# Two transformer layers in one kernel: a reordered opening of the first layer, and the last feed-forward pieces of the second layer spread over more turns

## The chip, the cores and the metric

The kernel runs on one core of one Trainium2 chip. Its time is the device time of one execution in microseconds (us); a kernel's figure is the median of its runs. The kernel before took 1442.1, 1445.23 and 1445.4 us, median 1445.23.

## The reference

`x` is 2048 tokens of width 128, in fp32. Two layers of the same shape follow one another, each with an attention part `s` and a feed-forward part `g`:

```
xn = layernorm(x)
s  = layernorm(xn + (relu_attention(xn) @ w_out + b_out)) * gamma + beta      # 16 heads of 8
g  = silu(routed_block(xn))
x  = x + s * g
xn = layernorm(x)
s  = causal_softmax_attention(xn, W_Q, W_K, W_V, W_O)                          # 16 heads of 64
g  = silu((silu(xn @ wg.T) * (xn @ wu.T)) @ wd.T)                              # hidden 384
x  = x + s * g

relu_attention: w = relu(q @ k.T / sqrt(8)); w / (sum(w) + 1e-6) @ v           # over all 2048 keys
routed_block:   the 255 tokens of highest router weight pass through a small transformer
                block and are written back scaled by that weight; the others pass unchanged
wg, wu, wd:     integers times 1/127
```

## The kernel before

**Engines and orders.** PE, ACT and DVE execute in the order in which the program is written (a manual schedule). POOL's and SP's (the DMA queue's) instructions are ordered by the Tile scheduler. Tokens are held as 16 chunks of 128 (`xin`, `xne`), taken together in four groups of 512.

**Opening of the first layer.** A group `i` is normalised by the generator `normalised(i)` in two parts. The first part takes the statistics on DVE (four pairs of `bn_stats`, `bn_aggr`) and the square root on ACT. The second takes the reciprocal and one Newton step, writes four chunks of `xne` (L895, all on DVE), transposes them on PE and copies the result on ACT (L102, L104). `begin()` runs this for the groups 0 and 1, with the projections of the keys of group 0 and of the first queries between them (`project`, L786: PE, then a rounded copy `high` on ACT and the remainder `low` added on DVE, L793), and the first values. All these projections are 512 columns wide. POOL meanwhile makes the copies of the weights that the projections read (L289 is one of its own for the routed block), and clears a buffer `nothing` of which SP later writes four copies to DRAM.

**Steps of the first layer.** The relu-attention runs in 256 steps, `n = 64 qc + 16 g + kb`: 512 queries `qc`, group of four heads `g`, block of 128 keys `kb`. A step issues four score matmuls (L948, one for each head of the group), four relus, each on ACT (L956) or DVE (L958) as a running account of work decides (`work.lesser`), and the products (L964) of the step two before. A group of heads needs its keys `kT[:, g]` for all 16 blocks. The keys of group 0 come straight from `project`; those of the groups 1 to 3 go in both halves (`high`, `low`) to DRAM (`spread`) and are read back by DMA into the rows where the scores want them. The rest of the opening is spread over the first steps by the tables

```
due = {
    0: (more_keys,), 1: (more, 2), 2: (all_keys, 2), 3: (more_values, 1), 4: (more, 3),
    5: (all_keys, 3), 6: (more_values, 2), 7: (all_keys, 1), 8: (all_queries, 0),
    9: (more_values, 3), 11: (all_keys, 0),
}
read = {9: (2, 1), 10: (3, 1), 12: (1, 1), 14: (0, 1)}
```

`more(i)` normalises group `i`, `all_keys(i)` makes its keys for all heads, `more_values(i)` its values, `more_keys` the keys of token group 1 for head group 0, and `read` starts the read-back of `kT`. A step that is not in `due` advances the generator `others()` instead: the routed block, then the second layer's feed-forward weights, then the end of each 512 queries. PSUM has six banks for scores and projections ("s"), one for those follow-ups that are not of that kind ("x"), and one accumulator.

**Turns of the second layer.** The causal attention runs in turns `r`, 19 for each of eight pairs of heads. A turn issues score matmuls (L1462), the masks and maxima on DVE (L1482, L1483), the exponentials on ACT (L1496), the transposes of the last turn's `p` (L1733), their evictions on ACT and DVE (L1740), and the weighing of the values (L1512). Into the turns a plan `ahead` puts the projections of keys (L1365), queries (L1415) and values (L1400) for coming turns. A projected key or query is copied by ACT (L1386) and split by POOL into a rounded part and a remainder (L1388, 64x512 casts, and L1390, subtractions).

**The last 512 tokens between the layers.** The feed-forward of the last 512 tokens isn't done before the turns begin. `tail()` lists its pieces, and the turn loop takes them one after the other: from turn 2 on one piece of arithmetic at the end of each turn (`first`, `gated`, `second`, `normal`), then from turn 6 on the pieces with a matmul in place of a projection (`turn` L1289, three gate and three up products L1294, `down` L1312). `first` and `second` take the moments of a tensor: statistics on DVE, then the inverse root from an integer first guess and four Newton steps of four small POOL instructions each (L1244 to L1248). `gated` has two parts of four DVE instructions: `y = (y - mean) * g` (L1267), then `xin = y * inv + xin` (L1271). `normal` writes the normalised tokens, which `turn` transposes.

Of the kernel before, what the change touches and what calls it, by code (L numbers as in the profile page):

```python
# [11 lines left out]
F32 = mybir.dt.float32  # L12
# [4 lines left out]
AF = mybir.ActivationFunctionType  # L17
# [5 lines left out]
P = 128  # L23
# [33 lines left out]
@with_exitstack  # L57
def mixed_layers_kernel(
    ctx: ExitStack,
    tc: tile.TileContext,  # L60
    a: dict,
    out: bass.AP,
):
    nc = tc.nc
    ctx.enter_context(nc.allow_non_contiguous_dma(reason="small weights and rows of sums"))

    const = ctx.enter_context(tc.tile_pool(name="const", bufs=1))
    small = ctx.enter_context(tc.tile_pool(name="small", bufs=4))


    ident = const.tile([P, P], F32, name="ident")
    make_identity(nc, ident)


    def row_load(name, n, pool):

        t = pool.tile([P, n], F32, name=f"row_{name}")
        nc.sync.dma_start(out=t, in_=a[name].partition_broadcast(P))
        return t


    xin = const.tile([P, NC, D], F32, name="xin")
    xn1T = const.tile([P, S], F32, name="xn1T")
    xsrc = a["x"].rearrange("(c p) d -> p c d", p=P)
    for i in range(NQ):
        nc.sync.dma_start(out=xin[:, 4 * i : 4 * i + 4, :], in_=xsrc[:, 4 * i : 4 * i + 4, :])


    with tc.manual_schedule(
        engines={mybir.EngineType.PE, mybir.EngineType.Activation, mybir.EngineType.DVE}  # L90
    ):
        second = layer1(ctx, tc, a, small, ident, xin, xn1T, row_load, out)
        layer0(ctx, tc, a, small, ident, xin, xn1T, row_load, second)
        for _ in second.turns:
            pass


def transposed(nc, psum, ident, src, dst, tag, bufs, copy):

    t = psum.tile([P, 4, P], F32, tag=tag, bufs=bufs, name="t")  # L100
    for i, s in enumerate(src):
        nc.tensor.transpose(t[:, i, :], s, ident)  # L102
    n = len(src)
    copy(dst, t[:, :n, :].rearrange("p a b -> p (a b)"))  # L104


def layer0(ctx, tc, a, small, ident, xin, xn1T, row_load, second):
    nc = tc.nc
# [11 lines left out]
    )  # L120
    nc.scalar.dma_start(
        out=w_qkv.rearrange("p g j t d -> p (g j t d)"), in_=a["w_qkv"]
    )

    w_k = keep.tile([P, 4, HD0, 4], F32, name="w_k")
    w_q = keep.tile([P, 4, HD0, 4], F32, name="w_q")
    for t, dst in ((1, w_k), (0, w_q)):
        for i in range(4):
            nc.gpsimd.tensor_copy(dst[:, :, :, i], w_qkv[:, 0, :, t, :])
# [9 lines left out]
    for n, bit in (("k", 2), ("q", 1)):  # L139
# [8 lines left out]
    w_out = end.tile([P, D], F32, name="w_out")  # L148
    nc.scalar.dma_start(out=w_out, in_=a["w_out"])
    b_out = row_load("b_out", D, end)  # L150
    gamma = row_load("gamma", D, end)
    beta = row_load("beta", D, end)
    router_w = keep.tile([P, 1], F32, name="router_w")
    nc.scalar.dma_start(out=router_w, in_=a["router_w"])
    router_b = row_load("router_b", 1, keep)
# [10 lines left out]
    rwb = rw.tile([P, KSEL], F32, tag="og", bufs=4, name="rwb")[:, :P]  # L166
    nc.gpsimd.tensor_copy(rwb, router_w.to_broadcast([P, P]))
    work = Work(nc)
    routed = routed_block(
        tc, a, work, rb, rw, dram, small, ps, ident, xne, xnT, g0, rwb, router_b, row_load,  # L170
        (b_out, gamma, beta, xin),
    )
# [45 lines left out]
def routed_block(  # L218
    tc, a, work, rb, rw, dram, small, ps, ident, xne, xnT, g0, rwb, router_b, row_load, rest
):  # L220
# [23 lines left out]
    yield  # L244

    tok = rb.tile([P, KSEL], BF16, name="tok")
    nc.gpsimd.iota(
# [515 lines left out]
def relu_attention(  # L763
# [18 lines left out]

    def project(dst, w, i, low):

        t = bank([P, 512], "s")
        nc.tensor.matmul(  # L786
            t, w.rearrange("p a d n -> p (a d n)"), xnT[:, 512 * i : 512 * i + 512],
            start=True, stop=True,
        )
        high = aw.tile([P, 512], F32R, tag="high", name="high")  # L790
        nc.scalar.copy(high, t)
        work.add(a=0.6, d=0.75)
        return lambda: nc.vector.scalar_tensor_tensor(dst, high, low, t, ALU.mult, ALU.add)  # L793

    def keys(i):
        return project(kT[:, 0, 512 * i : 512 * i + 512], w_k, i, low_k)

# [75 lines left out]

    def normalised(i):

        cs = range(4 * i, 4 * i + 4)
        st = small.tile([P, 4, 6], F32, tag="ln_st", name="ln_st")
        mv = small.tile([P, 4, 2], F32, tag="ln_mv", name="ln_mv")
        v = small.tile([P, 4], F32, tag="ln_v", name="ln_v")
        r = small.tile([P, 4], F32, tag="ln_r", name="ln_r")  # L880
        y = small.tile([P, 4], F32, tag="rs_y", name="y")
        t = small.tile([P, 4], F32, tag="rs_t", name="t")
        for k, c in enumerate(cs):
            nc.vector.bn_stats(st[:, k, :], xin[:, c, :])
            nc.vector.bn_aggr(mv[:, k, :], st[:, k, :])
        nc.vector.tensor_scalar(v, mv[:, :, 1], 1e-5, None, ALU.add)
        nc.scalar.activation(y, v, AF.Sqrt)
        yield
        nc.vector.reciprocal(y, y)
        nc.vector.tensor_tensor(t, y, y, ALU.mult)  # L890
        nc.vector.tensor_tensor(t, t, v, ALU.mult)
        nc.vector.tensor_scalar(t, t, -0.5, 1.5, ALU.mult, ALU.add)
        nc.vector.tensor_tensor(r, y, t, ALU.mult)
        for k, c in enumerate(cs):
            nc.vector.tensor_scalar(  # L895
                xne[:, c, 0:D], xin[:, c, :], mv[:, k, 0:1], r[:, k : k + 1],
                ALU.subtract, ALU.mult,
            )
        transposed(
            nc, ps, ident, [xne[:, c, 0:D] for c in cs], xnT[:, 512 * i : 512 * i + 512],  # L900
            "s", NS, nc.scalar.copy,
        )
        yield

    tokens = [normalised(i) for i in range(NQ)]

    def begin():

        next(tokens[0])
        next(tokens[1])  # L910
        next(tokens[0])
        k = keys(0)
        next(tokens[1])
        q = queries()
        k()
        next(tokens[2])
        q()
        values(0)
        work.a, work.d = 0.0, 3.0

    def more_keys():
        return keys(1)

    def more(i):

        next(tokens[i])
        work.add(a=0.6, d=2.0)
        if i + 1 < NQ:
            next(tokens[i + 1])
            work.add(a=0.2, d=1.8)  # L930

# [114 lines left out]
    def moments(src):  # L1046
# [18 lines left out]

    due = {
        0: (more_keys,), 1: (more, 2), 2: (all_keys, 2), 3: (more_values, 1), 4: (more, 3),
        5: (all_keys, 3), 6: (more_values, 2), 7: (all_keys, 1), 8: (all_queries, 0),
        9: (more_values, 3), 11: (all_keys, 0),
    }  # L1070
    read = {
        9: (2, 1), 10: (3, 1), 12: (1, 1), 14: (0, 1),
    }
# [17 lines left out]
    ends, steps, block = pools  # L1091
    ready, held, other, later = set(), [], others(), None
    begin()
    for n in range(n_steps + 2):
        if n < n_steps:
            held.append((n, scores(n)))
# [37 lines left out]
def layer1(ctx, tc, a, small, ident, x1, xn1T, row_load, out):  # L1134
# [94 lines left out]
    def moments(x):  # L1229
# [13 lines left out]
        nc.vector.tensor_scalar(yi, yi, -1.0, float(0x5F3759DF), ALU.mult, ALU.add)  # L1243
        for i in range(4):  # L1244
            nc.gpsimd.tensor_tensor(t, y, y, ALU.mult)
            nc.gpsimd.tensor_tensor(t, t, v, ALU.mult)
            nc.gpsimd.tensor_scalar(t, t, -0.5, 1.5, ALU.mult, ALU.add)
            nc.gpsimd.tensor_tensor(r if i == 3 else y, y, t, ALU.mult)  # L1248
        return mv, r

    def tail():
# [12 lines left out]
        def gated():  # L1264
            mv, r = got.pop()
            for c in range(4):
                nc.vector.scalar_tensor_tensor(  # L1267
                    y[:, c, :], y[:, c, :], mv[:, c, 0:1], g[:, c, :], ALU.subtract, ALU.mult
                )
            for c in range(4):  # L1270
                nc.vector.scalar_tensor_tensor(  # L1271
                    x[:, c, :], y[:, c, :], r[:, c : c + 1], x[:, c, :], ALU.mult, ALU.add
                )

        def second():
            got.append(moments(x))

        def normal():
# [38 lines left out]

        out = [(f, (), False) for f in (first, gated, second, normal)] + [(turn, (), True)]
        for n, later in (("w_gate", raw), ("w_up", times)):
# [341 lines left out]
    for pr in range(NP):  # L1661
# [5 lines left out]
        if pr == 0:  # L1667

            plan = [(0, values, 1)] + plan[6:]
        if pr == NP - 1:  # L1670
# [94 lines left out]
    def attention():  # L1765
# [10 lines left out]
        while r < len(turns) + 1 or todo or done or after:  # L1776
# [43 lines left out]
            for few in (r > 2, False, True, True)[: 4 if ending else 2]:  # L1820
# [5 lines left out]
                if f:  # L1826
                    f()
            if r >= 2 and pieces and not pieces[0][2]:
                g, args, _ = pieces.pop(0)
                g(*args)  # L1830
# [72 lines left out]
```

## Time and profile before

One profiled execution, whose own time is 1445.89 us; the span from its first to its last instruction is 1444.2 us. All rows below are of that execution.

| stretch of the span (us) | length | PE busy | DVE busy | ACT busy | POOL busy | granted clock |
|---|---|---|---|---|---|---|
| 0 to 18.59: up to the first scores | 18.59 | 6.83 | 13.26 | 4.58 | 9.51 | 1.00 |
| 18.59 to 43.99: steps 0 to 7 | 25.40 | 21.13 | 13.82 | 15.54 | 0.00 | 0.87 |
| 43.99 to 65.13: steps 8 to 15 | 21.14 | 19.02 | 12.26 | 12.38 | 0.00 | 1.00 |
| 65.13 to 505.00: the rest of the steps | 439.87 | 427.04 | 350.89 | 348.03 | 49.73 | 1.00 |
| 505.00 to 530.57: end of layer 1, turns 0 to 3 | 25.57 | 22.43 | 20.02 | 15.55 | 3.77 | 1.00 |
| 530.57 to 549.42: turns 4 and 5 | 18.85 | 12.60 | 15.46 | 8.04 | 9.34 | 0.82 |
| 549.42 to 1423.00: the other turns | 873.58 | 871.96 | 632.72 | 547.64 | 231.87 | 1.00 |
| 1423.00 to 1444.20: the end | 21.20 | 11.57 | 8.16 | 4.30 | 0.61 | 0.92 |
| whole span | 1444.20 | 1392.57 | 1066.60 | 956.05 | 304.83 | 0.993 |

A busy time counts the instructions that an engine executes, without register, branch, semaphore and DMA-issuing ones. The granted clock is the share of full speed at which TensorE was allowed to run in that stretch; a mean below 1 comes from windows at 0.50. In the timelines each line gives the start, the length, the engine and source line, the operation with the tile written and the tiles read, the shape, the number of instructions put together, and in brackets the idle time of the engine before it with what ended it.

### The profile page before, as it was taken

How to read it: one execution, taken by the hardware profiler on the slowest of the kernel's cores; microseconds unless marked ns; L12 is line 12 of the kernel's file. 1: busy time of each engine (PE TensorE's matmuls, PEld its weight loads, DVE VectorE, ACT ScalarE, POOL GpSimd, SP SyncE). 2: the span in 40 equal slices, each digit the busy share in tenths (PEclk: the TensorE clock that was granted, in tenths of full speed). 3: DMA queues.
4: the chain of work that ended last, by engine and by line, in shares of the span. 5: the costliest groups of instructions: out<-in, count | busy, mean ns of one | idle time of the engine just before them, and what ended most of it. 6: DMA issues, size and time to landing. Idle time of an engine off the chain costs nothing.

```text
span 1444.2 us, 26907 instructions
## 1 busy us (share of the span) xinstructions
PE 1392.6 (96%) x10070; PEld 845.5 (59%) x10070; DVE 1066.6 (74%) x1935; ACT 956.1 (66%) x2055; POOL 304.8 (21%) x414
## 2 busy tenths in 40 slices
PE   5999999999999979999999999999999999999997
PEld 2222333222222457777777777777777777777775
DVE  6588788788888476677768668768767767777775
ACT  4588787787888556666656666556656656666563
POOL 2001000150000121222232242242232232242210
PEclk9999999999999999999999999999999999999999
DMA  4432001111000311101111111011011111111110
GB/s 124 123 82 72 12 12 30 52 29 41 20 19 6 100 30 30 30 16 45 34 26 45 31 30 45 18 43 38 23 30 45 31 30 45 30 30 31 28 40 15
DMA packets 44065, 56.46 MB, mean 39 GB/s; under 512 B 11680, under 2 KB 26400, under 8 KB 43936
## 3 DMA queue, kind: packets, MB, share of 16 engines
q1 hardware_dynamic: 43120, 53.44, 14.6%
q8 instruction: 79, 1.29, 0.4%
q0 software_dynamic: 384, 1.05, 0.3%
q14 instruction: 50, 0.41, 0.1%
q10 hardware_dynamic: 432, 0.26, 0.1%
HBM read 27.74 MB, written 8.35 MB: 25 GB/s over the span
## 4 chain that ended last, share of the span: by engine, by line
PE 62%; ACT 1%; DVE 1%; issue 0%; ACTq 0%; DVEq 0%
PE t L1462 18%; PE z L1512 18%; PE t L1733 17%; PE m L1613 2%; PE m L1400 2%; PE m L1415 2%; PE m L1365 2%; ACT p L1496 1%; PE m L1294 0%; ACT pt L1740 0%; DVE xin L1271 0%; PE m L1312 0%; DVE zs L1596 0%; DVE res L1631 0%; ACT L1303 0%
## 5 line engine op out<-in xcount | busy, mean ns | idle before, releaser
L1483 DVE TENSOR_REDUCE tops<-t 128x1 f32<-128x1024 f32 (+4 forms) x320 | 334.6, 1062 | 98.9 <-PE t L1462 92.3
L956 ACT ACTIVATE rt<-t 128x512 f32<-128x512 f32 x597 | 315.5, 604 | 64.7 <-PE t L948 63.2
L1740 ACT COPY pt<-t 128x512 f32<-128x512 f32 (+3 forms) x359 | 163.4, 518 | 261.5 <-PE t L1733 260.3
L1496 ACT ACTIVATE p<-t,tops 128x1024 f32<-128x1024 f32 (+7 forms) x384 | 331.2, 883 | 7.8 <-DVE tops L1483 7.2
L958 DVE TENSOR_SCALAR rt<-t 128x512 f32<-128x512 f32 x427 | 275.7, 684 | 69.7 <-PE t L948 63.8
L1462 PE MATMUL t<-k,q 128*128 128x512 f32 (+4 forms) x1280 | 314.7, 389 | 9.4 <-ACT p L1496 9.3
L964 PE MATMUL t<-rt,va 128*9 128x512 f32 x2048 | 269.9, 600 | 4.3 <-ACT part L980 4.3
L1733 PE MATMUL t<-ident,p 128*128 128x128 f32 x2176 | 270.1, 275 | 2.6 <-ACT x L1386 1.4
L1512 PE MATMUL z<-pt,v 128*64 128x256 f32 (+1 forms) x2304 | 268.3, 374 | 0.5 <-ACT zs L1747 0.5
L1462 PEld LDWEIGHTS t<-k,q 128*128 128x128 f32 x1280 | 219.0, 189 | 83.2 <-issue 32.2
L1733 PEld LDWEIGHTS t<-ident,p 128*128 128x128 f32 x2176 | 244.2, 141 | 25.1 <-ACT pt L1740 4.3
L1512 PEld LDWEIGHTS z<-pt,v 128*64 128x64 f32 x2304 | 151.8, 136 | 86.7 <-issue 22.7
L948 PEld LDWEIGHTS t<-qT,kT 32*128 32x128 f32 x1024 | 63.1, 182 | 180.4 <-ACT rt L956 108.6
L1740 DVE COPY pt<-t 128x512 f32<-128x512 f32 (+3 forms) x289 | 163.6, 605 | 3.2 <-PE z L1512 2.0
L948 PE MATMUL t<-qT,kT 32*128 32x512 f32 x1024 | 152.7, 499 | 2.6 <-ACT rt L956 2.0
L1388 POOL CAST q<-x 64x512 fp32r<-64x512 f32 x60 | 36.5, 609 | 475.0 <-ACT x L1386 473.2
L1482 DVE TENSOR_TENSOR t<-t,mask_q 128x128 f32<-128x128 f32 (+1 forms) x192 | 64.8, 337 | 74.8 <-PE t L1462 68.6
L1496 ACT ACTIVATION_READ_ACCUMULATOR p<-t,tops 128x1 f32 x384 | 84.4, 220 | 0.0
L1390 POOL TENSOR_TENSOR q<-x,q 64x512 fp32r<-64x512 f32 x60 | 76.3, 1271 | 4.6
L1390 POOL TENSOR_TENSOR k<-x,k 64x512 fp32r<-64x512 f32 x60 | 76.2, 1271 | 4.6
L964 PEld LDWEIGHTS t<-rt,va 128*9 128x9 f32 x2048 | 30.7, 88 | 69.5 <-issue 60.1
L1388 POOL CAST k<-x 64x512 fp32r<-64x512 f32 x60 | 38.3, 638 | 127.0 <-ACT x L1386 125.2
(323 smaller groups left out, 934.4 us busy)
## 6 DMA issues: line engine op xcount, KB each, us to landing
q<-q SPq DMA_DIRECT2D x64, 256.0 KB
wide<-rows SPq DMA_DIRECT2D x90, 128.0 KB
qT<-spread SPq DMA_DIRECT2D x60, 64.0 KB
kT<-spread SPq DMA_DIRECT2D x48, 64.0 KB
spread<-high SPq DMA_DIRECT2D x8, 256.0 KB
spread<-low SPq DMA_DIRECT2D x8, 256.0 KB
rows<-xne SPq DMA_DIRECT2D x1, 1048.0 KB
xin<-in_x SPq DMA_DIRECT2D x4, 256.0 KB
```

Source lines behind the costliest of these rows:

```text
L948: nc.tensor.matmul(t, kT[rows, g, kb * P : (kb + 1) * P], qTs[qc, g][rows, :], start=True, stop=True,)
L956: nc.scalar.activation(rt, t, AF.Relu, scale=scale)
L958: nc.vector.tensor_scalar(rt, t, scale, 0.0, ALU.mult, ALU.max)
L964: nc.tensor.matmul(acc[32 * j : 32 * j + HD0 + 1, :], va[:, kb, 4 * g + j, :], r[j], start=(kb == 0), stop=(kb == NC - 1),)
L1388: nc.gpsimd.tensor_copy(high, x[half(e), :])
L1390: nc.gpsimd.tensor_tensor(low, x[half(e), :], high, ALU.subtract)
L1462: nc.tensor.matmul(flat[:, at_x : at_x + y - x], q[:, part, c4 * P : (c4 + 1) * P], k[:, x:y], start=(part == 0), stop=(part == 1),)
L1483: nc.vector.tensor_reduce(M[pr, c // 4][:, h, c % 4, es], x, axes, ALU.max, negate=True)
L1496: nc.scalar.activation(dst, x, AF.Exp, bias=M[pr, c // 4][:, h, c % 4, e : e + 1], accum_out=Z[pr, c // 4][:, h, c % 4, e : e + 1],)
L1512: nc.tensor.matmul(l1.z[half(e), slot, lo:2, :], V[pr, h][:, kb, half(e)], pts[e][:, kb, lo:2, :], start=(kb == 0), stop=(kb >= n0 - 1), s ...
L1733: nc.tensor.transpose(t[:, k + b, :], x[lo + b], ident)
L1740: copy(dst, t)
```

## The change

**Start of the first layer.** The first group of tokens is loaded in two DMAs of two chunks, ahead of all else on SP's queue; then come `w_qkv` (before on ACT's queue), the other three groups, and later `w_out` and `router_w`, which were on ACT's queue too. The weight copies for the queries are made before those for the keys. The broadcast copy `rwb` moves into the routed block, behind its first part. `normalised` is replaced by four functions: `stats(i, ks)` (the statistics of some of the four chunks), `root(i)`, `normal(i, engine)` and `turn(i)` (transposes and copy). `begin()` issues 36 transposes of the identity first and 6 more behind the first group (`fill`), takes the statistics of the first group alone, projects the queries before the keys, and cuts the follow-up of the first keys into the columns 0 to 127 and 128 to 511. The group 2 is transposed at step 3 and the group 3 at step 6; the arithmetic of the group 3 behind its statistics runs on POOL. The tables `due` and `read` change. POOL is put under the manual order as well from `begin()` up to step 16.

**Second layer.** Three Newton steps in place of four. `tail()` starts in turn 1 in place of turn 2, and its arithmetic is cut into six pieces: `first`, `gated`, `second` (the update of `xin`), `again` (the second moments), `rest` (nothing) and `normal`, so that `turn` can follow from turn 7 on. The last projections of the first pair (`queries`, `keys`, `values` of the last 512 tokens) go from the turns 7, 9, 11 to 8, 10, 12.

```diff
-    for i in range(NQ):
-        nc.sync.dma_start(out=xin[:, 4 * i : 4 * i + 4, :], in_=xsrc[:, 4 * i : 4 * i + 4, :])
+    for i in range(2):
+        nc.sync.dma_start(out=xin[:, 2 * i : 2 * i + 2, :], in_=xsrc[:, 2 * i : 2 * i + 2, :])
...
-    nc.scalar.dma_start(
+    nc.sync.dma_start(
         out=w_qkv.rearrange("p g j t d -> p (g j t d)"), in_=a["w_qkv"]
     )
+    for i in range(1, NQ):
+        nc.sync.dma_start(out=xin[:, 4 * i : 4 * i + 4, :], in_=xsrc[:, 4 * i : 4 * i + 4, :])
...
-    for t, dst in ((1, w_k), (0, w_q)):
+    for t, dst in ((0, w_q), (1, w_k)):
...
-    nc.scalar.dma_start(out=w_out, in_=a["w_out"])
+    nc.sync.dma_start(out=w_out, in_=a["w_out"])
...
-    nc.scalar.dma_start(out=router_w, in_=a["router_w"])
+    nc.sync.dma_start(out=router_w, in_=a["router_w"])
...
-    nc.gpsimd.tensor_copy(rwb, router_w.to_broadcast([P, P]))
...
     yield
 
+    nc.gpsimd.tensor_copy(rwb, router_w.to_broadcast([P, P]))
...
-    def project(dst, w, i, low):
+    def project(dst, w, i, low, cuts=(0, 512)):
...
-        nc.scalar.copy(high, t)
+        parts = [slice(*x) for x in zip(cuts, cuts[1:])]
+        for x in parts:
+            nc.scalar.copy(high[:, x], t[:, x])
         work.add(a=0.6, d=0.75)
...
+    def stats(i, ks):
         st = small.tile([P, 4, 6], F32, tag="ln_st", name="ln_st")
+        for k in ks:
+            nc.vector.bn_stats(st[:, k, :], xin[:, 4 * i + k, :])
+            nc.vector.bn_aggr(moment[:, i, k, :], st[:, k, :])
+
+    def root(i):
...
+        nc.vector.tensor_scalar(v, moment[:, i, :, 1], 1e-5, None, ALU.add)
+        nc.scalar.activation(y, v, AF.Sqrt)
...
+    def normal(i, engine):
...
         nc.vector.reciprocal(y, y)
+        engine.tensor_tensor(t, y, y, ALU.mult)
+        engine.tensor_tensor(t, t, v, ALU.mult)
+        engine.tensor_scalar(t, t, -0.5, 1.5, ALU.mult, ALU.add)
+        engine.tensor_tensor(r, y, t, ALU.mult)
+        for k in range(4):
+            c = 4 * i + k
+            engine.tensor_scalar(
+                xne[:, c, 0:D], xin[:, c, :], moment[:, i, k, 0:1], r[:, k : k + 1],
                 ALU.subtract, ALU.mult,
             )
+    def turn(i):
         transposed(
...
+    def fill(n):
+
+        t = bank([P, 4, P], "s")
+        for k in range(n):
+            nc.tensor.transpose(t[:, k % 4, :], ident, ident)
 
     def begin():
 
-        next(tokens[0])
-        next(tokens[1])
-        next(tokens[0])
-        k = keys(0)
-        next(tokens[1])
-        q = queries()
-        k()
-        next(tokens[2])
+        fill(36)
+        stats(0, range(4))
+        root(0)
+        stats(1, range(2))
+        normal(0, nc.vector)
+        turn(0)
+        fill(6)
+        stats(1, range(2, 4))
+        root(1)
+        (q,) = queries()
+        k_first, k_rest = keys(0, (0, P, 512))
+        stats(2, range(1))
+        normal(1, nc.vector)
+        turn(1)
         q()
+        k_first()
         values(0)
-        work.a, work.d = 0.0, 3.0
+        k_rest()
+        work.a, work.d = 0.0, 1.0
+
+    def more(i):
+        turn(i)
+        work.add(a=0.6)
+        if i == 2:
+            return lambda: moments_used(3, nc.gpsimd)
+
+    def moments_used(i, engine):
+        root(i)
+        normal(i, engine)
+        work.add(a=0.2, d=0.5)
 
     def more_keys():
-        return keys(1)
...
+        (k,) = keys(1)
+
+        def later():
+            k()
+            stats(2, range(1, 4))
+            moments_used(2, nc.vector)
+            work.add(d=2.8)
+
+        return later
+
+    def no_more():
+        work.add(d=1.7)
+        return lambda: stats(3, range(4))
...
     due = {
-        0: (more_keys,), 1: (more, 2), 2: (all_keys, 2), 3: (more_values, 1), 4: (more, 3),
-        5: (all_keys, 3), 6: (more_values, 2), 7: (all_keys, 1), 8: (all_queries, 0),
-        9: (more_values, 3), 11: (all_keys, 0),
+        0: (more_keys,), 1: (no_more,), 2: (more_values, 1), 3: (more, 2),
+        4: (all_keys, 2), 5: (more_values, 2), 6: (more, 3), 7: (all_keys, 3), 8: (all_keys, 0),
+        9: (all_queries, 0), 10: (more_values, 3), 11: (all_keys, 1),
     }
     read = {
-        9: (2, 1), 10: (3, 1), 12: (1, 1), 14: (0, 1),
+        9: (2, 1), 11: (3, 1), 12: (0, 1), 14: (1, 1),
     }
...
+    first = ExitStack()
+    first.enter_context(tc.manual_schedule(engines={mybir.EngineType.Pool}))
     begin()
     for n in range(n_steps + 2):
+        if n == 16:
+            first.close()
...
-        for i in range(4):
+        for i in range(3):
...
-            nc.gpsimd.tensor_tensor(r if i == 3 else y, y, t, ALU.mult)
+            nc.gpsimd.tensor_tensor(r if i == 2 else y, y, t, ALU.mult)
...
+        def second():
+            _, r = got.pop()
             for c in range(4):
                 nc.vector.scalar_tensor_tensor(
                     x[:, c, :], y[:, c, :], r[:, c : c + 1], x[:, c, :], ALU.mult, ALU.add
                 )
 
-        def second():
+        def again():
             got.append(moments(x))
+
+        def rest():
+            pass
...
-        out = [(f, (), False) for f in (first, gated, second, normal)] + [(turn, (), True)]
+        out = [(f, (), False) for f in (first, gated, second, again, rest, normal)] + [(turn, (), True)]
...
-            plan = [(0, values, 1)] + plan[6:]
+            plan = [(0, values, 1)] + plan[6:9] + [(8, queries, 3), (10, keys, 3), (12, values, 3)]
...
-            if r >= 2 and pieces and not pieces[0][2]:
+            if r >= 1 and pieces and not pieces[0][2]:
```

## The prediction

> **What bounds the kernel now.** I read the page first, then PE's timeline of the first 66 us, the busy-time table by stage, the waits of PE and DVE around the change of layers, and the timeline there.
>
> ```profile
> span 1444.2 us, 26907 instructions
> PE 1392.6 (96%) x10070; PEld 845.5 (59%) x10070; DVE 1066.6 (74%) x1935; ACT 956.1 (66%) x2055; POOL 304.8 (21%) x414
> PE   5999999999999979999999999999999999999997
> ```
>
> PE is busy for 1392.6 of 1444.2 us, so only its 51.6 idle us, and the time it runs at a low clock, can be won. PE's row of slices has three digits under 9: the start, the change of layers and the end. The change touches the first two.
>
> PE's timeline of the start (start, length, [idle before <- releaser]):
>
> ```profile
> 10.62 1.09 PE L102 MATMUL t<-ident,xne 128*128 128x128 f32 x4 [10.62 <-POOL fields L289]
> 12.47 2.05 PE L786 MATMUL t<-xnT,w_k 128*128 128x512 f32 x2 [0.77 <-ACT xnT L104]
> ...
> 18.59 0.51 PE L948 MATMUL t<-qT,kT 32*128 32x512 f32 x4 [0.38 <-DVE qT L793]
> 19.02 1.12 PE L786 MATMUL t<-xnT,w_k 128*128 128x512 f32 x2
> ...
> 23.86 1.15 PE L102 MATMUL t<-ident,xne 128*128 128x128 f32 x4 [2.61 <-DVE xne L895]
> ...
> 34.27 1.24 PE L102 MATMUL t<-ident,xne 128*128 128x128 f32 x4 [1.66 <-DVE xne L895]
> ```
>
> The first scores (step 0) start at 18.59, and the same projection takes 2.05 us before and 1.12 us after it: PE starts at half speed. Then PE waits twice for DVE to normalise the next 512 tokens. Each of these waits has a second price, in the granted clock (the column before the DMA share; the first columns are the stretch, its length and PE's busy time):
>
> ```profile
> 24.30:27.70 3.40, 3.40 (x16) 0.97 (x16) 1.81 (x10) 1.97 (x5) 0.00 (x0) 0.50 0.00 0
> 34.50:37.90 3.40, 3.40 (x16) 0.97 (x15) 1.18 (x3) 2.16 (x4) 0.00 (x0) 0.50 0.37 96
> 539.70:546.50 6.80, 4.58 (x13) 3.71 (x14) 6.46 (x20) 2.70 (x7) 0.40 (x2) 0.50 0.01 1
> ```
>
> The third row belongs to the change of layers, where the timeline shows why:
>
> ```profile
> 530.57 2.20 PE L1462 MATMUL t<-k,q 128*128 128x512 f32 x8
> ...
> 534.87 0.20 POOL L1248 TENSOR_TENSOR inv<-y,t 128x4 f32<-128x4 f32 x1
> 535.10 4.00 DVE L1271 SCALAR_TENSOR_TENSOR xin<-acc,inv,xin 128x128 f32<-128x128 f32 x4 [2.98 <-POOL inv L1248]
> 539.34 1.22 DVE L1483 TENSOR_REDUCE tops<-t 128x1 f32<-128x1024 f32 x1
> 541.92 3.78 PE L1462 MATMUL t<-k,q 128*128 128x512 f32 x8 [6.25 <-ACT p L1496]
> ```
>
> The scores of turn 4 are there at 532.8, but DVE takes their maximum only at 539.34: it stood 2.98 us waiting for POOL's Newton steps, then 4.00 us in four instructions that run beside POOL's casts (the four of L1267, nearly alone, took 1.19). ACT's exponentials wait for the maxima, PE for the banks they free: 6.25 us idle.
>
> **The start, by terms.** *Data.* w_qkv (192 KB, first on its queue) was in use by POOL at 3.91, the 256 KB of the first tokens by DVE at 4.67, both sharing the engines at 257 GB/s (2 to 4 us). Now the tokens go first, in two halves: I take 3.1 for the first half (bounds 2.7 and 4.7) and 5.3 for the second group, which now ends 704 KB (2.7 us at 257 GB/s) after the first packets at about 2 and lands some 0.5 later; before, it held nobody at 6.47, the other bound. The Trainium skill ("Trainium Kernel Development and Optimization", Key Constraints) says that queues share the same DMA engines and that a second issuer saves only issue time, which speaks against putting w_qkv on SP's queue: by it the second group is issued about 0.5 us later (SP's issues here take 0.43 to 0.51), and the sum would be 0.5 us worse.
>
> *Chain.* Four pairs of statistics take 1.7 (4.67 to 6.36), so the root is out at 5.2. Two pairs of the next group, 0.8, now stand ahead of the reciprocal in DVE's queue and wait for their data: 6.1. Reciprocal to r is 1.0 (8.58 to 9.58), four xne 1.1 (the row at 13.09; 1.47 at 9.58 beside POOL's memset, which is now queued on POOL behind the fourth group): 8.2. Last transpose and copy 0.9: xnT at 9.1, before at 12.33. Queries and keys 1.06 each on a warm PE, to 11.3; DVE, after the second group's normalisation (stats and root 1.4, chain 2.1 behind a root that ACT gives after its copy: to 11.6), makes qT in 0.75 and the first 128 keys in about 0.3; PE's transposes and values take 1.5 from 11.5. Step 0 at 13.0 to 13.3, before 18.59: **-5.3**. *Fills.* 36 transposes from about 1.5: at 0.21 each (10.62 to 17.3 ran so) they last until 8.8 or so, at 0.11 until 5.5; the chain needs PE at 7.5, so their price is 0 to 0.8, and I put 0.2 within the 13.3. By the skill ("TensorE: Matmul & The Clock Gate", What's actually happening) the gate judges free-running windows of about 3.4 us, so warm-up is a time and no count of matmuls, and a fixed 36 is right only by luck; an estimate by it: warm between 5.0 and 8.4, fills done between 7.2 and 8.8, the sum up to 0.7 us worse.
>
> *Steps 0 to 8* took 25.40 (18.59 to 43.99). Out of it go 4.27 idle (2.61 and 1.66), since the third group's transposes move from step 1 to 3, its DVE chain is over at about 21 and PE arrives at 21.6, and the fourth group's arithmetic moves to POOL; 3.4 of low clock (half of 6.8 busy us); and one projection (1.06, `all_keys(1)`, moved to step 11). Back come about 1.5: PE waits some 1.0 after step 1 for banks, and 0.4 for xnT of the third group, because ACT now stands at the third root (queued ahead of step 2's four ReLUs) until DVE has the statistics. On POOL the fourth group costs four small steps (0.28) and four xne at 0.61 (L714 has this form): 3.6 us, ready just as PE comes at 29. Steps 0 to 8: 25.4-4.3-3.4-1.1+1.5 = 18.1; I keep 18.5. Step 8 at 31.8 instead of 44.0.
>
> *Steps 8 to 16* took 21.14. The projection comes back (1.06); steps 7, 8, 9 now use the one "x" bank in a row, and each follow-up waits for DVE's `low` (1.02 and 1.10 in the trace), so one such wait more; one set of four transposes (0.6) falls behind step 16 and is owed: 22.7 with it. Sum at step 16: 12.2-1.6 = 10.6. I take off 1.1 for queues: POOL's memset of `nothing` now stands behind the fourth group and some 4.7 us of small POOL work (done about 33), and SP's queue holds its four 256 KB writes before kT's pieces: the first before the last blocks of group 0 (needed at step 12, about 44: no price), three (2 us of issue) before the first blocks of group 1, which land about 53.5 for step 16 at 54.5. Before, eight such reads were issued from 58.51 to 65.8 for a step at 65.1, so this was tight already; 0 to 2 us. **Start: -9.5**, bounds -4 (data late, clock low again) and -11.5.
>
> **The change of layers.** `first` moves to turn 1, where DVE is idle for 1.93 us before turn 2's mask; its 2.4 us there delay nobody, since ACT copies until 523.3. Newton has 12 instead of 16 POOL instructions (0.28 apart, so 1.1 us less) and runs from 522 to 525.5, ahead of the query casts (526.58), not behind them. `gated` (1.19) takes the place of the statistics in turn 2, the update of xin that of `gated` in turn 3: at 531 the query casts are over and the key casts, no longer behind Newton, start at 532. So 1.2 us, and the maxima of turn 4 are on time. From turn 4 to turn 6 PE took 18.85 (530.57 to 549.42) with 6.25 idle; at half clock it was busy 4.58, which gives back 2.3. New: the second statistics hold turn 5's maxima by about 2, of which 0.6 reaches PE, and 0.3 more in turn 4. 18.85-6.25-2.3+0.9 = 11.2: **-7.4**, with bounds -3.5 (the update still contends, 2.8 us more, and some of the clock loss) and -9. Fewer Newton steps alone: 0, POOL is 21% busy. The later turn of `normal`, `turn` and the nine pieces: 0; each meets the same pair of projections one turn later, and the four Silus with two table loads still cost the 1.38 us that PE waits at 581.25. Queries of the last tokens move from turn 7 to 8 and are needed in turn 11, two turns (14 us or more) later; copy, casts, DMA and landing took under 9 us (561.94 to 568.3 and some 2 to land). Without that cover turn 11 would wait one DMA, 2 us.
>
> **Sum.** Profiled execution 1445.89 (span 1444.2), which is 0.66 above the median of the runs: 1445.9-9.5-7.4 = 1429.0, on the scale of the median 1428.5.
>
> **Rivals.** *Only the layers' change pays:* the second group's data, or ACT standing at the third root, keeps PE idle enough for half clock, and the start gives 2 to 3: 1435. For it: one gap of 1.66 was enough at 34.3; against it: PE's queue is now fed by later steps. *Only the start pays:* the update still meets POOL's casts and ACT's copies bound turns 1 to 5 (PE was also idle 1.37 and 1.04 in turns 2 and 3 for ACT): -9.5-2, so 1434. *No change:* the wins are given back later in layer 0, where the routed work now falls one step later against the group ends (PE idles 12.8 us from 65 to 505): 1444. *Slower:* SP's queue stands at the first write of `nothing`; if POOL reaches its memset not at 33 but later than the need of step 12 (44 less 5 for issue and landing, so 39), each us more stops all scores, and the three later writes do the same at step 16. To end slower it must eat 17 us: POOL at 56, which its rows exclude unless its chain waits for something unseen; 1451.
>
> **How the numbers follow.** Both halves pay 0.66 (1423 to 1434), only the layers 0.10, only the start 0.09, no change 0.08, slower 0.07. 0.3% is 4.3 us, about what can be told from no change: faster 0.85, same 0.08, slower 0.07. The range 1422 to 1439 leaves out the last two cases and the edges.
>
> **What would show it.** Step 0's scores near 13.3, step 8's near 32, step 16's near 54.5; no granted clock of 0.50 from 24 to 38 on the old scale; DVE's update of xin at about 1.2 us with no wait for POOL; no PE gap over 2 us in turns 4 and 5; spans from step 16 to the layer's end, and after turn 8, as before. Wrong: a PE gap at step 12 or 16 released by a DMA, a first score after 15, or a wait of DVE for POOL in turn 3.

## The result, and the profile after

The changed kernel takes 1430.17 us (median of four runs, 1429.68 to 1431.19) against 1445.32 us (median of four runs of the kernel before): 15.15 us less, ratio 0.9896 with a 95% interval of 0.9877 to 0.9914. The forecast was 1428.5, range 1422 to 1439. The profiled execution took 1430.62 us, its span 1428.8.

The head of the page: PE's idle time is down from 51.6 to 33.9 us, and the start is the only slice that still has a digit under 9, besides the end.

```profile
span 1428.8 us, 26989 instructions
PE 1394.9 (98%) x10112; PEld 850.7 (60%) x10112; DVE 1061.3 (74%) x1930; ACT 953.1 (67%) x2054; POOL 307.5 (22%) x414
PE   8999999999999999999999999999999999999997
```

PE's timeline of the start (start, length, the releaser of an idle time in brackets):

```profile
1.49 6.08 PE L928 MATMUL t<-ident 128*128 128x128 f32 x36 [1.49 <-POOL ident masks.py:199]
8.72 1.10 PE L102 MATMUL t<-ident,xne 128*128 128x128 f32 x4 [1.15 <-DVE xne L913]
...
10.58 1.10 PE L789 MATMUL t<-xnT,w_q 128*128 128x512 f32 x2
...
14.08 0.51 PE L994 MATMUL t<-qT,kT 32*128 32x512 f32 x4
...
17.28 0.99 PE L994 MATMUL t<-qT,kT 32*128 32x512 f32 x3 [0.48 <-ACT rt L1002]
...
20.26 1.46 PE L994 MATMUL t<-qT,kT 32*128 32x512 f32 x4
...
57.12 0.50 PE L994 MATMUL t<-qT,kT 32*128 32x512 f32 x4 [1.34 <-DMA kT<-spread]
```

The first projection is warm (1.10 us, before 2.05), step 0 starts at 14.08 instead of 18.59, and the two waits for the normalisation of later groups (2.61 and 1.66) are gone. At step 16 (57.12) there is a new wait, 1.34 us for a DMA. The busy time by stage shows the clock (before the DMA share): 1.00, where before two windows had 0.50.

```profile
13.30:32.00 18.70, 18.22 (x116) 7.37 (x114) 14.20 (x42) 14.08 (x30) 5.31 (x14) 1.00 0.16 48
```

The timeline of the change of layers:

```profile
516.04 0.20 POOL L1300 TENSOR_TENSOR inv<-y,t 128x4 f32<-128x4 f32 x1
516.60 1.13 DVE L1319 SCALAR_TENSOR_TENSOR acc<-acc,mv,g 128x128 f32<-128x128 f32 x4
...
519.68 2.62 POOL L1448 TENSOR_TENSOR q<-x,q 64x512 fp32r<-64x512 f32 x2
...
521.65 1.58 DVE L1326 SCALAR_TENSOR_TENSOR xin<-acc,inv,xin 128x128 f32<-128x128 f32 x4
...
522.33 2.21 PE L1520 MATMUL t<-k,q 128*128 128x512 f32 x8
...
523.68 1.28 POOL L1446 CAST k<-x 64x512 fp32r<-64x512 f32 x2 [1.38 <-ACT x L1444]
```

The next two turns on PE, from its own timeline:

```profile
527.37 2.21 PE L1520 MATMUL t<-k,q 128*128 128x512 f32 x8
533.61 2.29 PE L1520 MATMUL t<-k,q 128*128 128x512 f32 x8 [0.48 <-ACT p L1554]
```

POOL has the inverse root at 516.24, five us before it is wanted. The update of `xin` (L1326) waits for nothing and takes 1.58 us instead of 4.00; it overlaps the last query subtraction (to 522.30) and is over when the key casts begin. The scores of turn 5 follow at 527.37 without a wait; of the 6.25 us of idle time 0.48 are left, one turn later.

Where the time went, between marks that both timelines have (first scores of a step or turn):

| stretch | before | after | difference | forecast |
|---|---|---|---|---|
| start to step 0 | 18.59 | 14.08 | -4.51 | -5.3 |
| step 0 to step 8 | 25.43 | 19.25 | -6.18 | -6.9 |
| step 8 to step 16 | 21.09 | 23.79 | +2.70 | +2.7 (1.6, and 1.1 for queues) |
| step 16 to turn 1 | 450.19 | 449.78 | -0.41 | 0 |
| turn 1 to turn 4 | 15.27 | 15.43 | +0.16 | 0 |
| turn 4 to turn 6 | 18.85 | 11.28 | -7.57 | -7.4 |
| turn 6 to the end | 894.76 | 895.22 | +0.46 | 0 |
| span | 1444.18 | 1428.83 | -15.35 | -16.9 |

### The profile page after: what moved, and what is told of

It reads as the page before. It is cut to its first block, busy times and chain, and to the rows that moved or that the text cites. A ratio compares the mean times of both kernels' runs of the same rounds, so it can differ in the third digit from the quotient of the medians.

```text
span 1428.8 us, 26989 instructions
## 1 busy us (share of the span) xinstructions
PE 1394.9 (98%) x10112; PEld 850.7 (60%) x10112; DVE 1061.3 (74%) x1930; ACT 953.1 (67%) x2054; POOL 307.5 (22%) x414
## 4 chain that ended last, share of the span: by engine, by line
PE 62%; ACT 1%; DVE 1%; issue 0%; DVEq 0%; ACTq 0%
PE t L1520 18%; PE z L1570 18%; PE t L1791 16%; PE m L1671 2%; PE m L1473 2%; PE m L1458 2%; PE m L1423 2%; ACT p L1554 1%; PE m L1352 0%; ACT pt L1798 0%; PE m L1370 0%; DVE tops L1541 0%; DVE zs L1654 0%; DVE res L1689 0%; ACT L1361 0%
## 5 line engine op out<-in xcount | busy, mean ns | idle before, releaser
L994 PE MATMUL t<-qT,kT 32*128 32x512 f32 x1024 | 155.9, 496 | 2.8 <-DMA kT<-spread 1.3
```

The lines of the kernel that those rows point to most:

```text
L994: nc.tensor.matmul(t, kT[rows, g, kb * P : (kb + 1) * P], qTs[qc, g][rows, :], start=True, stop=True,)
```

## The experiments

Single executions of one kernel differ by more than many of these effects, so the verdicts below rest on marks inside the traces; only three of the experiments (each half alone, and the three edits at the end) were timed more than once.

**The two halves, each alone.** The first layer's edits on the kernel before; then the second layer's.

> The first layer's edits alone; the second layer's tail, Newton steps and plan as before. Theory (the two halves are independent and add up): step 0's scores near 14.1, step 16's near 57.1 as in the changed kernel, the last step's scores about 8.4 earlier than before (468.9), and then the change of layers as before: PE idle 6.25 us in turn 4, a clock of 0.50 there. Span 1444.2 - 8.4 = 1435.8, time near 1437. Rival (the start's gain is given back later in layer 0, only the change of layers pays): time within 2 us of 1445.

> The second layer's edits alone (tail in six pieces from turn 1, three Newton steps, first pair's plan); the opening as before. Theory: step 0 at 18.6 and the last step at 477.3 as before, then from the scores of turn 4 to those of turn 6 some 11.3 us in place of 18.85, no wait of DVE for POOL, no clock of 0.50 near 540; 7.2 to 7.6 us less: time near 1438. Rival (the layers' half pays only because the earlier start moved the clock's windows or the queues): 3 us or less, time over 1442.

Start alone: 1436.68 against 1446.34, ratio 0.9935 (0.9919 to 0.9952). Step 0 at 13.38, step 16 at 56.24, last step at 467.97, and then the old change of layers, with its idle time of 6.22 us and its clock of 0.50. Layers alone: 1441.16, ratio 0.9958 (0.9942 to 0.9974). Step 0 at 18.77; from turn 4 to turn 6 it is 11.28 us, as in the changed kernel, with no wait of DVE for POOL (timeline of the layers alone):

```profile
533.21 1.56 DVE L1275 SCALAR_TENSOR_TENSOR xin<-acc,inv,xin 128x128 f32<-128x128 f32 x4
533.86 2.20 PE L1469 MATMUL t<-k,q 128*128 128x512 f32 x8
538.88 2.21 PE L1469 MATMUL t<-k,q 128*128 128x512 f32 x8
```

The product of the two ratios is 0.9893, the change as a whole has 0.9896: the halves add up, and the gain of the start isn't given back. The time of the layers alone is 3 us over what was expected. Of these, 1.0 lies in the kernel before, which took 1446.34 beside it, and the profile shows why a part of the rest is not the edit's: steps 0 to 16 took 47.8 us, 1.3 more than in the kernel before, with a low clock for two windows at 23 instead of one.

**Newton steps.** Three steps alone on the kernel before; four steps in the changed kernel.

```diff
-        for i in range(4):      # kernel before, r if i == 3
+        for i in range(3):      # r if i == 2; the second experiment undoes this in the changed kernel
```

> The kernel before with three Newton steps in place of four, nothing else. Theory from the trace of before: there DVE stands 2.98 us waiting for POOL's result, so four POOL instructions less (4 x 0.28) bring the update, the maxima and the scores of turn 4 forward by 1.1 us: PE idle 5.1 instead of 6.25, DVE idle before the update 1.9; the update still takes 4 us beside POOL's casts. Rival (the prediction's own words, 'fewer Newton steps alone: 0'): nothing moves by more than 0.3.

> The changed kernel with four Newton steps again, all else as changed. Theory: the root is out at 517.2 instead of 516.1 and is wanted at 521.65, before the query casts that start at 518.3; the span up to turn 8 moves by less than 0.3. Rival (the fewer steps are what frees the update): the update waits for POOL again, 1 us or more between turns 3 and 5.

With three steps in the kernel before, its timeline shows the update still at 4.00 us, but started earlier:

```profile
538.06 4.00 DVE L1271 SCALAR_TENSOR_TENSOR xin<-acc,inv,xin 128x128 f32<-128x128 f32 x4 [1.85 <-POOL inv L1248]
...
544.88 3.78 PE L1462 MATMUL t<-k,q 128*128 128x512 f32 x8 [5.10 <-ACT p L1496]
```

DVE's wait falls by 1.13 us (from 2.98), PE's by 1.15 (from 6.25), and turns 4 to 6 take 18.11 instead of 18.85: there the step count was on the path. The one run as a whole took 1449.28 us, against 1442.18 to 1449.09 for the kernel before, so this gain shows in the marks alone. In the changed kernel four steps cost nothing: turns 1 to 6 take 26.71 us with three and with four (turn 4 to turn 6 11.28 and 11.29). So the fewer steps are not what frees the update.

**The tail from turn 2.** `if r >= 2` again, the six pieces as changed.

> The changed kernel with its six pieces begun in turn 2 instead of turn 1; each piece one turn later. Theory: the first statistics (2.4 us on DVE) now stand ahead of turn 3's maxima, where DVE had no idle time to spare, the Newton steps are queued behind the query casts on POOL (to 522.3) but still end before turn 4; the update falls at the end of turn 4, after the key casts (527.7), and takes 1.2 to 1.6: no half clock, 0.5 to 1.5 us more between turns 2 and 6, nothing else. Rival (the early start is what the whole gain of the layers' half rests on): the update meets casts or waits for POOL again, 3 us or more, with a clock of 0.50.

The update stands at 527.36, at the end of turn 4, and takes 2.16 us; turns 2 to 6 take 22.05 us (22.30 in the changed kernel), the turn after that 0.65 more, and from turn 1 to the last turn it is 896.62 us against 896.17. No low clock, no wait for POOL. Both the theory's price in turns 2 to 6 and the rival fell: the early start is worth some 0.5 us at most, by this one execution. The step count, the turn in which `first` runs and the plan of the first pair (below) being ruled out, what remains of the edit is that the update stands one turn behind `gated`, with the root already there and clear of most casts. This cut was not run by itself.

**Without the fills.** `fill(36)` and `fill(6)` left out.

> The changed kernel without the 42 filling transposes. Theory (they pay by the clock): PE's first work is the first group's transposes near 8, and it runs cold for some 6.8 us after that as in the kernel before, so each projection takes 2.05 us instead of 1.06: step 0 about 2 us later than with them (13.1 to 14.1 in three executions so far), near 15.5 to 16, the rest of the opening later by the same. Rival (the fills only occupy PE, and the chain on DVE sets step 0): step 0 by 14.2 at the latest.

PE's timeline:

```profile
7.72 1.16 PE L102 MATMUL t<-ident,xne 128*128 128x128 f32 x4 [7.72 <-DVE xne L913]
9.64 2.05 PE L789 MATMUL t<-xnT,w_q 128*128 128x512 f32 x2 [0.77 <-ACT y L899]
11.48 1.51 PE L789 MATMUL t<-xnT,w_k 128*128 128x512 f32 x2
...
14.26 0.51 PE L992 MATMUL t<-qT,kT 32*128 32x512 f32 x4
```

The queries take 2.05 us, cold, the keys 1.51, half cold. Step 0 comes at 14.26; the execution to set beside it is the one with four Newton steps, where the second group's tokens came at the same time (5.23, here 5.24) and step 0 at 13.06. In this pair of executions the fills are worth 1.2 us, neither the theory's 2 nor nothing: PE was warm within 5 us of its first work, not 6.8. Their price: in ten executions with fills they went from the cold to the warm spacing (0.21 to 0.11 us) anywhere between 4.3 and 7.5, and the 36th, in nine of them, started between 6.7 and 8.3.

**The second group's statistics behind.**

```diff
-        stats(1, range(2))
         normal(0, nc.vector)
+        stats(1, range(2))
```

> The changed kernel with the second group's first two statistics issued behind the normalisation of the first group, one line moved. Theory (DVE, in order, stands for the second group's DMA before it can take the reciprocal of the first): the reciprocal follows ACT's root (5.2) at once instead of at 7.1, the first group's xne are written by 7.4, and step 0 comes 1.2 to 1.5 earlier, near 12. Rival (PE is the bound there: 36 fills end at 7.6, and POOL's copies beside DVE make xne slower): gain under 0.7.

The reciprocal now follows the root (5.12), and yet step 0 comes at 13.08. PE's fills, cold until 7.5 in this execution, let the first transposes start only at 8.38, and on DVE the statistics that were moved come later at their full length, ahead of the second group's normalisation. In this one execution the rival was right. With the order as changed, step 0 came between 13.06 (tokens of the second group at 5.23) and 14.08 (at 6.30).

**w_qkv on ACT's queue.** `nc.scalar.dma_start` for this one load.

> The changed kernel with w_qkv back on ACT's queue, all else as changed. Theory (one issuer fewer costs the second group 0.5 us): the second group is there at about 5.8 instead of 6.3, the first by 4.2 instead of 3.8 since it shares the engines with w_qkv; the reciprocal and step 0 come 0.3 to 0.5 earlier. Rival (the tokens ahead of the weights are what counts): the first group's statistics end at 5.7 or later instead of 4.75, and step 0 is no earlier, or up to 0.5 later.

DVE's timeline (the first tokens, the second group, the first reciprocal):

```profile
4.09 0.29 DVE L892 BATCH_NORM_STATS2 ln_st<-xin 128x6 f32<-128x128 f32 x1 [1.32 <-DMA xin<-in_x]
...
5.89 0.45 DVE L892 BATCH_NORM_STATS2 ln_st<-xin 128x6 f32<-128x128 f32 x1
...
6.90 0.15 DVE L906 RECIPROCAL y<-y 128x4 f32<-128x4 f32 x1
```

The first tokens come 1.0 later (4.09 instead of 3.06), DVE, busy until then, comes to the second group at 5.89 without a wait, the reciprocal is at 6.90 (6.05 to 7.12 in the runs with the order as changed) and step 0 at 13.64, in the middle of theirs. The rival was right: the first group loses 1.0. Whether the second group gains isn't shown, as 5.89 lies within the 5.2 to 6.3 of the other executions.

**The writes of zeros.** Three of the four writes to `back` stand in SP's queue ahead of the key reads of step 16. The experiment moves the writes behind that of the routed rows in the program:

```diff
-    for i in range(NQ):
-        nc.sync.dma_start(out=back[...], in_=nothing)
 ...
     nc.sync.dma_start(out=rows..., in_=xne[:, :, 0:131])
+    for i in range(NQ):
+        nc.sync.dma_start(out=back[...], in_=nothing)
```

SP's queue in the changed kernel (start, length of the issuing):

```profile
50.12 2.05 SPq L307 DMA_DIRECT2D back<-nothing  x3
52.21 8.28 SPq L843 DMA_DIRECT2D kT<-spread  x12
```

> The changed kernel with the four writes of zeros to the buffer back moved behind the write of the routed rows, long after step 16. Theory (three of them, 2.05 us of issue on SP's queue, stand ahead of the key reads of step 16): these reads are issued 2 us earlier, step 16's wait of 1.2 to 1.34 us for kT goes, step 16 comes 22.6 to 22.8 us after step 8 in place of 23.5 to 23.8. Rival (the keys' own write to DRAM, not the queue, sets it): a wait of 0.8 or more stays at step 16.

And in the experiment:

```profile
49.95 4.93 SPq L843 DMA_DIRECT2D kT<-spread  x8
54.93 1.72 SPq L342 DMA_DIRECT2D back<-nothing  x3
```

The scheduler moved the three writes by 5 us only, but behind eight of the twelve reads, which are issued from 49.95 on. Step 16's wait is gone, and it comes 22.12 us after step 8 instead of 23.45 to 23.79: 1.3 to 1.7 us. That the three writes held step 16 is shown.

**POOL's order and the fourth group.** Two experiments: POOL left to the scheduler in the opening (with the first pair's last projections back at turns 7, 9, 11); and the fourth group's arithmetic on DVE.

```diff
-    first.enter_context(tc.manual_schedule(engines={mybir.EngineType.Pool}))
```
```diff
-            return lambda: moments_used(3, nc.gpsimd)
+            return lambda: moments_used(3, nc.vector)
```

> The changed kernel with POOL left to the scheduler in the opening (no manual order), and, far from it in time, the first pair's last projections back at turns 7, 9, 11. POOL's memsets and tables now run from about 8 to 17, beside the normalisation of the first two groups, and all four writes of zeros are issued on SP's queue near 13, ahead of every read of kT. Theory (POOL's work beside DVE's fp32 SBUF instructions slows these, as xne took 1.47 instead of 1.11 in the kernel before; the writes were what held step 16): the xne of the two groups take 1.4 to 2.5 each instead of 1.11, step 0 comes 0.5 to 1.5 later than the 13.1 to 14.1 of the other runs, and step 16's wait of 1.2 to 1.3 for kT goes: step 16 within 1 of 56.4. Rival (POOL's order is worth nothing): xne at 1.1 and step 0 as before, step 16 near 55. Plan: turns 6 to 13 take the same time within 0.3; rival: 1 us or more.

> The changed kernel with the fourth group's arithmetic on DVE instead of POOL. Theory (the move to POOL takes load off the engine that the relus wait for): DVE gets 2 us more (0.9 for the root's steps, 1.1 for four xne) ahead of relus near 26, PE waits 0.5 to 1.7 us more in steps 4 to 6 and step 8 comes that much later (19.25 to 19.9 us after step 0 so far); with a wait over 1.6 a window at 0.50 is added, 1.7 more. Rival (DVE has room there): step 8 within 0.3.

POOL free: the xne of the two groups took 1.12 and 1.29, hardly slower, since POOL itself stood until 10.21 for `router_w`; step 0 at 13.81, steps 8 to 16 22.06 us, no wait at step 16. The slowing was small (the 1.29 is the group beside POOL's tables; in the next experiment that group took 1.47 beside them), the queue's part was there. Turns 6 to 13 took 50.74 us against 50.76: the plan of the first pair moves nothing there.

Fourth group on DVE: step 8 comes 19.60 us after step 0. This execution has a window of low clock at 18.0; with the group on POOL it was 19.84 to 19.90 in five executions with such a window and 19.25 to 19.29 in four without. So DVE has room, and is if anything 0.2 us faster; the theory fell. And step 16 has no wait, 22.12 us after step 8, because POOL now reaches the memset at 15 and SP writes the zeros when its queue is empty. POOL's timeline and SP's queue:

```profile
15.06 0.53 POOL L305 MEMSET nothing<- 128x512 f32 x1
```

```profile
15.62 2.31 SPq L307 DMA_DIRECT2D back<-nothing  x4
```

In the changed kernel the memset stands at 34.81, behind the fourth group. So the move to POOL gains nothing in the steps, and costs 1.3 to 1.7 us at step 16. The time of this one run, 1433.29, doesn't show it: low clock from 154.5 on makes steps 64 to 128 3.0 us longer than in the changed kernel, and low clock at 574.4 makes turn 11 1.6 us longer (10.80 instead of 9.18).

**Three edits at once**: writes behind, statistics behind, `fill(28)`.

> Three edits on the changed kernel: the writes of zeros moved behind the write of the routed rows, the second group's first statistics behind the first group's normalisation, and 28 fills instead of 36. Theory: fills end between 6.4 and 7.4, the first transposes start at 7.0 to 7.5, step 0 at 12.0 to 12.5 whenever the second group lands, step 16 at 54.0 to 54.5: 2 to 2.5 us earlier than in the changed kernel, time 1427.5 to 1428.5. Rival (28 fills are too few where the clock's windows fall late): PE still cold at its first projection (2.05 instead of 1.06 us), step 0 at 13 or later.

It took 1429.34 (four runs, 1427.79 to 1433.13) against 1447.19 for the kernel before measured beside it, ratio 0.9874 (0.9857 to 0.9890). The interval overlaps that of the changed kernel (0.9877 to 0.9914), so it is not shown to be faster. Step 16 came at 55.44, in place of 56.2 to 57.1; the expected 54.5 was missed because step 0 came at 13.45. The second group's transposes, which stand ahead of step 0 in PE's queue, had to wait for DVE (PE's timeline):

```profile
11.52 1.10 PE L102 MATMUL t<-ident,xne 128*128 128x128 f32 x4 [0.40 <-DVE xne L913]
```

So once the data wait is gone, DVE's work on two groups sets step 0. This profiled execution is the 1433.13 one. A part of what lengthened it (3.0 us in steps 64 to 128) shows in the busy times of one stretch (clock before the DMA share), with the three edits:

```profile
154.50:161.50 7.00, 6.93 (x33) 1.90 (x37) 3.32 (x5) 4.72 (x11) 0.00 (x0) 0.51 0.00 1
```

and in the changed kernel:

```profile
154.50:161.50 7.00, 6.49 (x48) 2.33 (x44) 6.29 (x10) 7.00 (x17) 0.00 (x0) 1.00 0.03 6
```

## Why the prediction was right, and where it was off

**The sum.** Forecast -16.9 on the span, measured -15.35; both halves pay, as the likeliest case said. The two cases in which only one half pays, and the one without a change, are excluded by the runs of the halves alone.

**The change of layers** was right in place, cause and size: 11.28 us from turn 4 to turn 6, forecast 11.2 (which is 7.65 less; the sum entered 7.4). The update took 1.58 instead of the 1.2 forecast, as its first instructions still meet the last query subtraction. The statement that fewer Newton steps alone are worth nothing holds in the changed kernel and not in the one before, where they were worth 0.7 us. That the pieces after that cost nothing was nearly right: 0.46 us from turn 6 to the end. Section "Who interferes with whom" of the Trainium skill's page "SBUF — State Buffer" states that a DVE instruction with two SBUF inputs contends with a GpSimd instruction that reads SBUF; the 4.00, 2.16 and 1.58 us of the same four instructions, beside casts and subtractions throughout, for a part, and at their edge, agree.

**The start** has two terms that were off, both to the same side in this execution. Of its edits the fills, the place of the second group's statistics, the queue of `w_qkv`, POOL's order and the engine of the fourth group were run alone; that the later transposes give the two idle times back is read from the trace, and from the fourth group on DVE, where no wait for it came back.

*Data.* The first tokens came at 3.06 (forecast 3.1). The second group's came at 6.30, not 5.3, and DVE stood 1.34 us for them ahead of the first reciprocal, which was forecast at 6.1 and came at 7.12 (DVE's timeline, changed kernel):

```profile
6.30 0.29 DVE L892 BATCH_NORM_STATS2 ln_st<-xin 128x6 f32<-128x128 f32 x1 [1.34 <-DMA xin<-in_x]
...
7.12 0.14 DVE L906 RECIPROCAL y<-y 128x4 f32<-128x4 f32 x1
```

This is a spread between executions: in eight executions with the same order of loads it was used from 5.2 to 6.3 on. Step 0 came at 13.06 to 14.08, the forecast 13.3 lies inside. Step 16 came at 56.24 to 57.12 in four such executions and at 65.11 to 66.56 in three with the old opening; the means are 9.2 us apart, forecast 9.5.

*Steps 0 to 8.* The clock and the two idle times were given back as worked out, but 18.5 us became 19.25. The step that failed is "back come about 1.5" for PE's waits after step 0. From 15.57 to 18.20 PE did eight score matmuls that take 0.9 us elsewhere, and those of the steps 3 and 4 took until 21.66 and 24.11, 1.40 and 0.89 instead of 0.44: 1.7, 1.0 and 0.4, together some 3 us of waits, mostly too short for the timeline to print as gaps. The releasers that the trace names are ACT's relus. ACT stood at the third root, ahead of the relus of step 2 (ACT's timeline, changed kernel):

```profile
19.52 0.21 ACT L899 ACTIVATE y<-ln_v 128x4 f32<-128x4 f32 x1 [1.80 <-DVE ln_v L898]
```

The prediction named this stand, but took 0.4 us for it. That the clock came back whole is luck of this execution: six of the ten with fills have a window of low clock at 17.6 to 18.5, and steps 0 to 8 then take 19.60 to 19.90, 0.3 to 0.6 more.

*Steps 8 to 16* came out at the forecast, 23.8, and for the reason given, SP's three writes before the reads; that the figure fits so well is luck. Without the wait the stretch takes 22.1 us (four experiments), not 22.7, and the writes cost 1.3 to 1.7, not 1.1. The prediction listed a wait for a DMA at step 16 among the signs that it would be wrong, while it had put 1.1 us for just this in its sum; the sign was badly chosen, and "step 16's near 54.5" doesn't follow from the sum either, which gives 55.6. The prediction saw that the memset stands behind the fourth group on POOL (done about 33 by it, started at 34.81 in the trace). What it had wrong is that it counted the fourth group's move to POOL as a gain in the steps before; that gain is not there.

**The fills** were priced at 0 to 0.8 us. The section "What's actually happening" of the page "TensorE: Matmul & The Clock Gate" says that warm-up is a time in free-running windows, not a count. The spread of the warm point from 4.3 to 7.5 us, with the first fill at 1.49 in each execution, agrees in that no count of fills marks it (14 to 28 of them were cold); but the prediction's estimate from the page, 5.0 to 8.4, lies too late: three of ten executions were warm before 5.0, two of them about 2.9 us after the first fill. The 36 fills ended ahead of the data in the execution of the tables above and up to 1 us behind it in others (8.4 against 7.4 with four Newton steps). The granted clock reads 1.00 up to 18.59 in the table of the kernel before, although projections of 2.05 us ran at half speed there: ahead of the first warm point only the matmuls' own times show the clock.

## What to carry to other kernels

Look for an engine that stands between two others at a change of stages. Here DVE waited for sixteen tiny POOL instructions and then ran beside POOL's casts; letting the result lie for a turn was worth more than making it shorter. When work is moved to an engine "with room", list what else that engine has to issue, down to the memset that a DMA waits for in a queue where reads for later steps are lined up. And in an opening of a few microseconds, an order is worth only what the next bound leaves: data, fills and DVE's work were within 1 us of each other, and mending one of them moved step 0 hardly at all.

## What the runs showed of the hardware

A 3.4 us window of low clock falls into a run or not by its phase, with the program unchanged in that stretch. In each execution the low windows start a whole multiple of 3.41 us after the point at which PE got warm (with four Newton steps 17.71 after 7.47, three times 3.41). In the ten executions with fills this grid has a line 3.9 to 4.7 us after step 0 in the six that have a low window there, at 17.6 to 18.5, and at 3.4, 5.1, 5.7 and 6.3 us in the four that have none. In the changed kernel and its variants, steps 64 to 128 took 124.9 us in six executions without such a window, 126.3 to 126.5 in three with one near 155, and 127.9 in two with two: 1.5 us for each. A few such windows more or less would make up the 4 to 7 us by which executions of most kernels differ here (the first layer's edits alone: 1435.08 to 1439.8, the kernel before beside them: 1442.18 to 1449.09); that was not followed run by run. It is why marks inside a trace were needed to settle effects of 1 us.

What POOL does beside DVE sets DVE's price. Of the four instructions of the update of `xin`, the two beside POOL's casts took 0.65 and 0.74 us in the kernel before, and the two beside its subtractions 1.42 and 1.41; in the changed kernel the last three, with POOL idle, took 0.34 each.
